# A four-layer graph network on one core: two pools for a strip's weights, an earlier read-back of the in-degrees, another queue for one load, and another layout of four scratch tables

## The chip, the cores and the metric

The kernel runs on one core of a Trainium2 chip. A time is the device time of one execution in microseconds (us); a kernel's time is the median of its runs. The profile is one further execution, with its own time. TensorE is PE in the profile (its weight loads are PEld), VectorE is DVE, ScalarE is ACT, GpSimd is POOL and SyncE is SP. "SPq" and "POOLq" are the queues in which SP and POOL issue DMAs.

## What is computed

6250 nodes with 128 features each, and 206250 directed edges, sorted by destination (100000 pairs in both directions and a loop at each node). Each layer normalises the nodes, sums rows over the edges and adds the result to x:

```python
h = relu(layernorm(x))
x = x + leaky_relu(neighbor @ W1.T + b1 + (h * neighbor) @ W2.T + b2)   # neighbor = sum of edge_weight * h[src] over dst
h = relu(layernorm(x))                                                  # called h1 below
agg = segment_sum(h[src], dst) / maximum(in_degree, 1)
f = gelu(agg @ Wl.T + bl + h @ Wr.T)
x = x + graph_norm(f) + h                                               # one graph: mean and variance over all nodes
h = relu(layernorm(x))
x = x + mean over edges of x_clique @ W.T + b                           # summed over dst, by src
h = relu(layernorm(x))
x = x + GRU(h @ W_in, messages summed over dst) @ W_out + b_out
```

## The kernel before, in words

The graph becomes a dense matrix of counts (how often node s sends to node d), 49 blocks of 128 nodes by 49. It is made once and used in three layers.

**First stage: 25 strips** (`strip`, L857). A strip is two blocks of destinations (256 nodes; the last, number 24, has one block). For each destination the edges' sources and weights are gathered (`prepare`, L637, indirect DMAs on POOL's queue), DVE makes one-hot tiles (L724 to L727), PE multiplies them (L746), and ACT copies two results out: the counts as bytes (`cnt`, L755, then to DRAM as `cnt_d`, L882) and the weighted sums of a strip (`edge_w`, L753, 49 x 256 floats, 50,176 bytes in a partition). `prepare` also counts the in-degrees into `deg` (L678, L685); the last of them comes while strip 23 runs. Layer 0's products of a strip (`layer0`, L775, matmuls L783) run during the next strip; `finish0` (L804) ends layer 0 for a strip and writes three scratch tables: `h_d` (h1), `u_d` (x + h1) and `f_d` (h1 @ Wr.T + bl). For the last strips these writes are on POOL's queue, before that on SP's (L807). Strips 1 to 23 stand inside `tc.manual_schedule()`: each engine takes them in the order of the code. Strip 0 and everything from strip 24 to the end of the first stage stand outside it, and the framework's planner orders their instructions by its own estimate of when each is ready.

**Second to fourth stage: three dense layers** (`dense`, L928, run by L1257 to L1300, inside a second `manual_schedule`). A layer goes through chunks of four blocks of destinations. In layer 1 a chunk takes five loads of `cnt_d` into a ring of three tiles (L954), each feeding two steps; DVE and ACT turn the bytes into floats in `wide` (L966 on DVE, L968 on ACT; both also sum the row into `deg2`), and PE does 98 matmuls into `acc` (L985). Its other operand is h1, split into two parts (`h_parts`). During the first chunk alone, `h_up_to` (L1031) brings h1 from `h_d` by groups of four blocks (13 groups, 256 KB each, three buffers `h`), and DVE splits each group (L587 and L588, "halves"): groups 0 to 2 before the chunk, 3 and 4 ahead of its step q=10, 5 to 7 ahead of q=20, 8 and 9 ahead of q=30, 10 to 12 ahead of q=40.

**Order on the queues at the seam.** Small loads are "chores" between the steps. On SP the second stage begins: the ring's first load (L954), the weight `WlT` (L1051), the in-degrees (`inverse_degrees`, L1056: read `deg_d` back, node by node, 4 bytes each, 6400 of them, and let DVE invert them at L1059 and L1060), h1's groups 3 and 4 (L1035), the ring's second load, and so on. On POOL: two memsets (L1260, L1261). `deg_d` is written from `deg` (3200 runs of 8 bytes) at L910.

**Memory.** The pools of the first stage are closed at its end, and those of the later stages lie over them. Going by the tiles' sizes, the pool `late` (deg2, inv1, WlT, f_sum and others) lies over `keep`, `work` (with finish0's tiles) and the first of the two `edge_w` buffers; the ring lies wholly over the second `edge_w` buffer, which holds the odd strips; `wide` lies over that and the pools after it.

Of the kernel before, what the change touches and what calls it, by code (L numbers as in the profile page):

```python
# [9 lines left out]
F32 = mybir.dt.float32  # L10
# [3 lines left out]
ALU = mybir.AluOpType  # L14
DVE = mybir.EngineType.DVE

P = 128
D = 128
N = 6250
NB = -(-N // P)  # L20
NR = N - (NB - 1) * P
NPAD = NB * P
# [444 lines left out]
SB = 2  # L467
SW = SB * P
STRIPS = [(k, min(SB, NB - k * SB)) for k in range(-(-NB // SB))]
NS = len(STRIPS)  # L470
# [20 lines left out]
def fast(ctx: ExitStack, tc: tile.TileContext, a: dict, out: bass.AP, flag: bass.AP):  # L491


    nc = tc.nc
    const = ctx.enter_context(tc.tile_pool(name="f_const", bufs=1))
    dram = ctx.enter_context(tc.tile_pool(name="f_dram", bufs=1, space=bass.MemoryType.DRAM))
# [3 lines left out]
    make_identity(nc, ident)  # L500
    identh = const.tile([P, P], BF16, name="f_identh")
    nc.vector.tensor_copy(identh, ident)
    ones = const.tile([P, P], F32, name="f_ones")
    nc.vector.memset(ones, 1.0)
    node0 = const.tile([P, NS], F32, name="f_node0")
# [23 lines left out]

    cnt_d = dram.tile([NCH, P, CB, NPR * P], U16, name="cnt_d")  # L530
    cntT_d = dram.tile([P, NQB, NPR * P], U16, name="cntT_d")
    u_d = dram.tile([NPAD, D], F32, name="u_d")
    f_d = dram.tile([NPAD, D], F32, name="f_d")
    h_d = dram.tile([NPAD, D], F32, name="h_d")
    x_d = dram.tile([NPAD, D], F32, name="x_d")
    smp_d = dram.tile([NSMP, 1], I32, name="smp_d")
    deg_d = dram.tile([NS, P, WN], F32, name="deg_d")

    def rows(table, g, nb):
        return table[g * P : (g + nb) * P, :].rearrange("(b p) f -> p b f", p=P)  # L540
# [50 lines left out]
    with ExitStack() as bx:  # L591
        def pool(name, bufs):
            return bx.enter_context(tc.tile_pool(name="b_" + name, bufs=bufs))
# [18 lines left out]

        deg = keep.tile([P, NS, WN], F32, name="deg")
        h0 = keep.tile([P, NB, D], F32, name="h0")
        work, edge = pool("work", 1), pool("edge", 2)
        xpool = pool("x", 2)

        def norms():
# [185 lines left out]
        def finish0(g, nb, agg):  # L804

            w = nb * P
            queue = nc.sync if g < (NS - 3) * SB else nc.gpsimd  # L807
            pt = turned_rows(h0[:, g : g + nb, :], nb)
            inter = work.tile([P, SW], F32, name="inter")
            nc.vector.tensor_mul(by_half(inter, nb), by_half(agg, nb), pt)  # L810
            xs = work.tile([P, SB, D], F32, name="xs0", bufs=2)
            load_x(xs, g, nb)
            yield
            po = banks.tile([P, SW], F32, name="po", tag="pK")
            for j in range(nb):
                s = slice(j * P, (j + 1) * P)
                nc.tensor.matmul(po[:, s], agg[:, s], w1, start=True, stop=False)  # L817
                nc.tensor.matmul(po[:, s], inter[:, s], w2, start=False, stop=True)  # L818
            full = work.tile([P, SW], F32, name="full")
            nc.vector.tensor_add(full[:, :w].rearrange("p (b f) -> p b f", f=D),  # L820
                                 po[:, :w].rearrange("p (b f) -> p b f", f=D), bcast(b12, nb))
            nc.vector.scalar_tensor_tensor(full[:, :w], full[:, :w], 0.2, full[:, :w],
                                           op0=ALU.mult, op1=ALU.max)
            nc.vector.tensor_add(flat(xs[:, :nb, :]), flat(xs[:, :nb, :]), full[:, :w])
            h1 = work.tile([P, SB, D], F32, name="h1")
            yield from norm(xs, h1, nb)
            nc.gpsimd.tensor_tensor(xs[:, :nb, :], xs[:, :nb, :], h1[:, :nb, :], op=ALU.add)
            queue.dma_start(rows(h_d, g, nb), h1[:, :nb, :])
            queue.dma_start(rows(u_d, g, nb), xs[:, :nb, :])
            yield  # L830
            pt = turned_rows(h1, nb)
            ht = work.tile([P, SW], F32, name="ht0")
            nc.scalar.copy(by_half(ht, nb), pt)
            yield
            pf = banks.tile([P, SW], F32, name="pf", tag="pK")
            for j in range(nb):
                s = slice(j * P, (j + 1) * P)
                nc.tensor.matmul(pf[:, s], ht[:, s], wr, start=True, stop=True)  # L838
            fs = work.tile([P, SB, D], F32, name="fs")
            nc.vector.tensor_add(fs[:, :nb, :], pf[:, :w].rearrange("p (b f) -> p b f", f=D),  # L840
                                 bcast(bl, nb))
            queue.dma_start(rows(f_d, g, nb), fs[:, :nb, :])

# [10 lines left out]

        def strip(k, nb):  # L857
            nonlocal before, edges, by_edge, hots
            edge_w = edge.tile([P, NB, SW], F32, name="edge_w")
            end = ends.pop() if ends else iter(())  # L860
            last, piece, following = nb * P // WN, 0, None
            for w0 in range(0, last, PW):
                if w0 % TW == 0:
                    now, t1 = hots, w0 + TW
                    if t1 < last:
                        hots = one_hots(by_edge, t1)
                    elif following:
                        hots = one_hots(following, 0)
                if w0 // PW % PT == PT // 2:
                    if piece in END_AT:  # L870
                        next(end, None)
                    if piece in EDGES_AT:
                        following = next(edges, None)
                if w0 * WN % P == 0:
                    cnt = cnts.tile([P, NPR, P], U16, name="cnt")
                count(w0, now, cnt, edge_w)
                if k and w0 // PW % 2:
                    next(before, None)
                g, w1 = k * SB + w0 * WN // P, w0 + PW
                if w1 * WN % P == 0:  # L880
                    c, i = CHUNK_OF[g]
                    nc.sync.dma_start(cnt_d[c, :, i, :], flat(cnt))  # L882
                if w1 % (PW * PT) and w1 < last:
                    continue
                if not k:
                    next(before, None)
                if piece == NEXT_AT and k + 2 < NS:
                    edges = prepare(k + 2)
                    next(edges)
                for _ in range(TURN_AT.count(piece) if k else 0):  # L890
                    next(turns, None)
                piece += 1
            by_edge = following
            for _ in chain(before, end):
                pass
            before = layer0(k, nb, edge_w)

        strip(*STRIPS[0])
        with tc.manual_schedule():
            for k, nb in STRIPS[1:-1]:  # L900
                strip(k, nb)
        strip(*STRIPS[-1])
        end = ends.pop()
        for _ in before:
# [2 lines left out]
            pass  # L907


        nc.sync.dma_start(deg_d.rearrange("s p w -> p s w"), deg)  # L910
        found = small.tile([P, 1], F32, name="found")
        nc.vector.tensor_reduce(found, deg, axis=mybir.AxisListType.XY, op=ALU.add)
        p_all = psum.tile([1, 1], F32, name="pL")
# [117 lines left out]
    def h_up_to(q):  # L1031
        while to_split and to_split[0][0] < q:
            g, nb = to_split.pop(0)
            h = whole.tile([P, GB, D], F32, name="h")
            nc.sync.dma_start(h[:, :nb, :], rows(h_d, g, nb))  # L1035
            halves(nc.vector, [h_parts[:, g : g + nb, i, :] for i in range(2)], h[:, :nb, :])

    deg2 = late.tile([P, NCH, NB], F32, name="deg2")
    inv1 = late.tile([P, NS * SB], F32, name="inv1")
    wl, wc, w_in, w_msg, w_out = (late.tile([P, D], F32, name="f_" + n)  # L1040
                                  for n in ("WlT", "WcT", "W_inT", "W_msg", "W_outT"))
    w_ih, w_hh = (late.tile([P, 3 * D], F32, name="f_" + n) for n in ("W_ihT", "W_hhT"))
# [10 lines left out]
    def load_row(t, n):  # L1053
        return lambda: nc.sync.dma_start(t, a[n].to_broadcast([P, D]))

    def inverse_degrees():  # L1056
        with nc.allow_non_contiguous_dma(reason="one number for each node, once"):
            nc.sync.dma_start(inv1, deg_d.rearrange("s p w -> (s p w)").rearrange("(b p) -> p b", p=P))
        nc.vector.tensor_scalar(inv1, inv1, 1.0, None, op0=ALU.max)  # L1059
        nc.vector.reciprocal(inv1, inv1)  # L1060

    def load_f(g, nb):
        return lambda: nc.sync.dma_start(f[:, g : g + nb, :], rows(f_d, g, nb))

# [90 lines left out]
    def end2(g, nb, acc):  # L1157
        w = nb * P
# [3 lines left out]
        pa = times(agg, wc, nb)  # L1162
        x = work.tile([P, CB, D], F32, name="x", bufs=3)
        xg, fg = x[:, :nb, :], f[:, g : g + nb, :]
        nc.sync.dma_start(xg, rows(u_d, g, nb))
        nc.gpsimd.tensor_tensor(xg, xg, bcast(b_res, nb), op=ALU.add)
        nc.vector.tensor_mul(fg, fg, bcast(gain, nb))
        yield
# [16 lines left out]
        for _ in steps:  # L1185
            pass
        nc.gpsimd.tensor_tensor(xg, xg, bcast(b_out, nb), op=ALU.add)
        nc.gpsimd.dma_start(rows(x_d, g, nb), xg)
        yield
        pt = psum2.tile([P, CB * P], F32, name="pT")  # L1190
        for j in range(nb):
# [18 lines left out]
    def end3(g, nb, acc):  # L1210
# [23 lines left out]
        new = work.tile([P, CB * P], F32, name="wd")  # L1234
        nc.scalar.activation(new[:, :w], r[:, :w], AF.Tanh, bias=b_ih[:, 2:3])
        x = work.tile([P, CB, D], F32, name="x", bufs=3)
        nc.sync.dma_start(x[:, :nb, :], rows(x_d, g, nb))
        yield
        keep_h = hh[:, cols]
        nc.vector.tensor_sub(keep_h, keep_h, new[:, :w])  # L1240
# [16 lines left out]
    with tc.manual_schedule():  # L1257
        n1 = 2 * NPR // KP
        chores = [[] for _ in range(NCH * n1)]
        chores[0] += [load(wl, "WlT"), lambda: nc.gpsimd.memset(f_sum, 0.0)]  # L1260
        chores[1] += [inverse_degrees, lambda: nc.gpsimd.memset(sq_sum, 0.0)]  # L1261
        for c, (g, nb) in enumerate(CHUNKS):
            chores[c * n1 + (7 if c == 0 else 2)].append(load_f(g, nb))
        for i, g in enumerate(range(0, NQB, GB)):
# [95 lines left out]
```

## Time and profile before

| | us |
|---|---|
| median of 7 runs (lowest 1909.02, highest 1918.71) | 1912.54 |
| the profiled execution | 1916.7 |
| its span, first to last instruction | 1914.9 |
| PE, DVE, ACT, POOL busy | 1796.4, 1409.3, 1205.0, 456.2 |
| first stage: strips and layer 0 | 0 to about 1036 |
| layer 1, first chunk | 1036.8 to about 1071 |
| layer 1, a later chunk | 23.1 each |
| layers 2 and 3 | from about 1350, to the end |

The page gives busy times by engine, 40 slices of the span, DMA queues, the chain of work that ended last, and the costliest groups. Its line numbers are those of the listing above. A busy PE includes time at a lower granted clock, so the clock ("PEclk") has to be read beside it. In an answer by windows, a line has the window, its length, each engine's busy time with the number of instructions, the granted clock, the share of the DMA engines' time and GB/s. A line of waits has the sum, the number of times and the longest.

### The profile page before, as it was taken

What the parts mean: (1) busy time and instruction counts of PE and PEld (TensorE: products, weight loads), DVE (VectorE), ACT (ScalarE), POOL (GpSimd) and SP (SyncE); (2) the same over time, 40 slices, a digit from 0 to 9 for tenths busy, and PEclk for the clock granted to TensorE, in tenths of its full rate; (3) what the DMA queues carried; (4) which work ended last, traced back from release to release, by engine and by line L of the source; (5) the groups of instructions that cost most, each with busy time, mean ns of one, the idle gap of its engine ahead of it and who ended that gap; (6) DMA issues with size and microseconds to landing.
All of it is one profiled execution on the core that took longest, in us unless ns stands there. A gap on an engine that the chain in (4) does not pass through costs nothing.

```text
span 1914.9 us, 65340 instructions
## 1 busy us (share of the span) xinstructions
PE 1796.4 (94%) x28172; PEld 1504.9 (79%) x28172; DVE 1409.3 (74%) x2943; ACT 1205.0 (63%) x2834; POOL 456.2 (24%) x412
## 2 busy tenths in 40 slices
PE   0799999999999999999986999999899999999996
PEld 0688888888888888888875788888677877777774
DVE  5888888888888888888843776776888755444453
ACT  2877777777777777777752676776555554434442
POOL 3134333433343334323401011000523210000000
PEclk9899999999999999999988999999999999999998
DMA  3236454546454645553213654654445454434441
GB/s 74 79 88 135 109 140 100 140 104 134 101 132 106 132 102 130 109 132 86 83 50 87 198 165 137 198 149 123 122 127 149 130 155 141 125 101 151 133 145 46
DMA packets 299742, 232.04 MB, mean 121 GB/s; under 512 B 111184, under 2 KB 288451, under 8 KB 299443
## 3 DMA queue, kind: packets, MB, share of 16 engines
q1 hardware_dynamic: 290627, 213.46, 42.1%
q0 software_dynamic: 7952, 13.91, 2.5%
q8 instruction: 223, 3.65, 0.8%
q10 hardware_dynamic: 864, 0.39, 0.3%
q14 instruction: 76, 0.62, 0.1%
HBM read 130.53 MB, written 76.70 MB: 108 GB/s over the span
## 4 chain that ended last, share of the span: by engine, by line
PE 83%; DVE 7%; issue 4%; DMA 2%; ACT 2%; POOL 0%; SPq 0%; POOLq 0%; DVEq 0%; ACTq 0%
PE acc L985 31%; PE pL L783 29%; PE pK L746 15%; DVE wide L946 1%; PE pf L838 1%; PE po L817 1%; PE pA L1105 1%; DVE x L1175 1%; DVE fh L1132 1%; PE po L818 1%; DMA smp_d<-in_dst 1%; DVE agg L789 1%; ACT h L575 1%; PE pM L1202 0%; PE pA L1247 0%
## 5 line engine op out<-in xcount | busy, mean ns | idle before, releaser
L783 PE MATMUL pL<-edge_w,h 64*128 64x256 f32 (+1 forms) x4900 | 620.3, 388 | 4.7 <-DVE agg L789 1.0
L985 PE MATMUL acc<-wide,parts 128*128 128x512 f32 (+1 forms) x2548 | 583.8, 388 | 11.5 <-DVE wide L966 10.7
L985 PEld LDWEIGHTS acc<-wide,parts 128*128 128x128 f32 x2548 | 464.0, 189 | 116.6 <-issue 14.8
L755 ACT CAST cnt<-pK 128x400 uint8<-128x400 f32 x784 | 396.3, 506 | 204.4 <-PE pK L746 188.6
L783 PEld LDWEIGHTS pL<-edge_w,h 64*128 64x128 f32 x4900 | 436.4, 188 | 46.6 <-DVE agg L789 6.7
L746 PEld LDWEIGHTS <-s_hot 64*128 64x128 bf16 x18816 | 372.8, 95 | 73.2 <-issue 21.1
L746 PE MATMUL pK<-k_hot,s_hot 64*128 64x49 bf16 (+1 forms) x18816 | 389.9, 193 | 24.7 <-ACT edge_w L753 12.5
L753 ACT COPY edge_w<-pK 128x392 f32<-128x392 f32 x784 | 399.1, 509 | 0.0
L727 DVE TENSOR_TENSOR k_hot<-k_hot,by_edge 128x2352 bf16<-128x2352 bf16 x196 | 271.8, 1387 | 8.0
L724 DVE TENSOR_TENSOR s_hot<-iota,keys 128x2048 bf16<-128x2048 bf16 x196 | 239.5, 1222 | 45.6 <-PE pK L746 42.5
L966 DVE TENSOR_SCALAR_CACHE_REDUCE wide<-ring 128x512 fp32r<-128x512 uint8 (+1 forms) x325 | 193.1, 651 | 41.3 <-ACT wide L968 19.3
L968 ACT ACTIVATE wide<-ring 128x512 fp32r<-128x512 uint8 (+1 forms) x312 | 184.9, 596 | 54.7 <-ACT wide L968 32.5
L634 POOL DMA_INDIRECT dst<-in_dst,off_i x50 | 82.6, 1652 | 400.5 <-DVE node L672 383.7
L985 PE MATMUL acc<-wide,q_parts 128*128 128x512 f32 (+1 forms) x650 | 162.0, 399 | 12.8 <-DVE wide L946 12.5
L961 ACT CAST wide<-ring 128x1024 fp32r<-128x1024 uint8 (+3 forms) x130 | 120.9, 957 | 73.9 <-PE acc L985 71.4
L960 DVE CAST wide<-ring 128x1536 fp32r<-128x1536 uint8 (+1 forms) x130 | 119.9, 948 | 54.3 <-PE acc L985 40.7
L985 PEld LDWEIGHTS acc<-wide,q_parts 128*128 128x128 f32 x650 | 116.8, 191 | 44.5 <-DVE wide L946 17.5
L726 DVE TENSOR_TENSOR k_hot<-iota,keys 128x800 bf16<-128x800 bf16 x196 | 126.5, 645 | 0.0
L1251 POOL DMA_DIRECT2D out<-x x12 | 10.2, 851 | 324.0 <-DVE x L1249 324.0
L1230 DVE SCALAR_TENSOR_TENSOR wb<-pT,f_b_hh,wb 128x512 f32<-128x512 f32 (+1 forms) x13 | 9.4, 720 | 100.4 <-PE pT L1227 100.4
L1013 POOL TENSOR_TENSOR f_sum<-f_sum,fh 128x512 f32<-128x512 f32 (+2 forms) x13 | 16.5, 1271 | 279.4 <-ACT fh L1118 237.7
L634 POOL DMA_INDIRECT src<-in_src,off_i x50 | 77.6, 1551 | 15.2 <-issue 14.6
(167 smaller groups left out, 1565.3 us busy)
## 6 DMA issues: line engine op xcount, KB each, us to landing
ring<-cnt_d SPq DMA_DIRECT2D x120, 640.0 KB
cnt_d<-cnt SPq DMA_DIRECT2D x49, 800.0 KB
cntT_d<-tt SPq DMA_DIRECT2D x125, 160.0 KB
ring<-cntT_d SPq DMA_DIRECT2D x60, 320.0 KB
xs<-in_x SPq DMA_DIRECT2D x12, 256.0 KB
xs<-in_x SPq DMA_DIRECT2D x24, 128.0 KB
h<-h_d SPq DMA_DIRECT2D x12, 256.0 KB
fh<-f_d SPq DMA_DIRECT2D x12, 256.0 KB
```

What stands on the lines that cost most here:

```text
L634: nc.gpsimd.indirect_dma_start(out=t, out_offset=None, in_=col[name], in_offset=bass.IndirectOffsetOnAxis(ap=idx, axis=0))
L724: nc.vector.tensor_tensor(s_hot, count_up(P), at(0, P), op=ALU.is_equal)
L726: nc.vector.tensor_tensor(k_hot[:, :, 0], count_up(NBP), at(1, NBP), op=ALU.is_equal)
L727: nc.vector.tensor_tensor(k_hot[:, :, 1:, :NB], k_hot[:, :, :1, :NB].to_broadcast([P, tq, 3, NB, TI]), parts.to_broadcast([P, tq, 3, NB, T ...
L746: nc.tensor.matmul(pk[:, h, to], s_hot[r, u, :, t], rhs, start=j == 0, stop=True, skip_group_check=True)
L753: nc.scalar.copy(m.rearrange("p b (i h) -> p b i h", h=WN), by_block[:, 1, :NB])
L755: nc.scalar.copy(m.rearrange("p b e (i h) -> p b e i h", h=WN), by_block[:, 0].rearrange("p (b e) i h -> p b e i h", e=2))
L783: nc.tensor.matmul(pl[:, h, :w], h0[r, s, :], edge_w[r, s, :w], start=s == 0, stop=s == NB - 1)
L961: nc.scalar.copy(to[:, 3:ks], of[:, 3:ks])
L966: nc.vector.tensor_scalar(to[:, k], of[:, k], 1.0, None, op0=ALU.mult, op1=ALU.add, accum_out=total)
L968: nc.scalar.activation(to[:, k], of[:, k], AF.Copy, accum_out=total)
L985: nc.tensor.matmul(acc[:, : nb * P], parts[:, s, j, :], rhs, start=s + j == 0, stop=s == end and j == 1)
```

## The change

`inv1` moves to the pool of constants, and its read-back to a place ahead of strip 24, outside `manual_schedule`, with the write of `deg_d` in front of it; the chore is gone. The two `edge_w` buffers become two pools of one buffer each, taken in turn. h1's groups are issued by POOL instead of SP. The four scratch tables of nodes by features are laid out partition by partition, `[128, 49, 128]` instead of `[6272, 128]`, so that a transfer of several blocks has one run of 1 KB (two blocks) or 2 KB (four blocks) for each partition, where it had runs of 512 bytes.

```diff
+    inv1 = const.tile([P, NS * SB], F32, name="inv1")
...
-    u_d = dram.tile([NPAD, D], F32, name="u_d")
-    f_d = dram.tile([NPAD, D], F32, name="f_d")
-    h_d = dram.tile([NPAD, D], F32, name="h_d")
-    x_d = dram.tile([NPAD, D], F32, name="x_d")
+    u_d = dram.tile([P, NB, D], F32, name="u_d")
+    f_d = dram.tile([P, NB, D], F32, name="f_d")
+    h_d = dram.tile([P, NB, D], F32, name="h_d")
+    x_d = dram.tile([P, NB, D], F32, name="x_d")
...
-        work, edge = pool("work", 1), pool("edge", 2)
+        work = pool("work", 1)
+        edge = [pool(n, 1) for n in ("edge0", "edge1")]
...
-            queue.dma_start(rows(h_d, g, nb), h1[:, :nb, :])
-            queue.dma_start(rows(u_d, g, nb), xs[:, :nb, :])
+            queue.dma_start(h_d[:, g : g + nb, :], h1[:, :nb, :])
+            queue.dma_start(u_d[:, g : g + nb, :], xs[:, :nb, :])
...
-            edge_w = edge.tile([P, NB, SW], F32, name="edge_w")
+            edge_w = edge[k % 2].tile([P, NB, SW], F32, name="edge_w")
...
         with tc.manual_schedule():
             for k, nb in STRIPS[1:-1]:
                 strip(k, nb)
+        nc.sync.dma_start(deg_d.rearrange("s p w -> p s w"), deg)
+        with nc.allow_non_contiguous_dma(reason="one number for each node, once"):
+            nc.sync.dma_start(inv1, deg_d.rearrange("s p w -> (s p w)").rearrange("(b p) -> p b", p=P))
+        nc.vector.tensor_scalar(inv1, inv1, 1.0, None, op0=ALU.max)
+        nc.vector.reciprocal(inv1, inv1)
         strip(*STRIPS[-1])
...
-        nc.sync.dma_start(deg_d.rearrange("s p w -> p s w"), deg)
...
-            nc.sync.dma_start(h[:, :nb, :], rows(h_d, g, nb))
+            nc.gpsimd.dma_start(h[:, :nb, :], h_d[:, g : g + nb, :])
...
-    inv1 = late.tile([P, NS * SB], F32, name="inv1")
...
-    def inverse_degrees():
...
-        chores[1] += [inverse_degrees, lambda: nc.gpsimd.memset(sq_sum, 0.0)]
+        chores[1].append(lambda: nc.gpsimd.memset(sq_sum, 0.0))
```

The other reads and writes of `u_d`, `f_d` and `x_d` (L841, L1063, L1165, L1188, L1237) change their index in the same way and stay on their queues.

More of the change, by code (lines that the diff above doesn't have):

```diff
@@ L841, in finish0 @@
                                  bcast(bl, nb))
-            queue.dma_start(rows(f_d, g, nb), fs[:, :nb, :])
+            queue.dma_start(f_d[:, g : g + nb, :], fs[:, :nb, :])
         for by_edge in prepare(0):
@@ L1054, in load_row @@
         return lambda: nc.sync.dma_start(t, a[n].to_broadcast([P, D]))
-    def inverse_degrees():
[L1057 to L1060, printed above, removed]
     def load_f(g, nb):
-        return lambda: nc.sync.dma_start(f[:, g : g + nb, :], rows(f_d, g, nb))
+        return lambda: nc.sync.dma_start(f[:, g : g + nb, :], f_d[:, g : g + nb, :])
     q_parts = late.tile([P, NQB, 2, D], F32R, name="q_parts")
@@ L1164, in end2 @@
         xg, fg = x[:, :nb, :], f[:, g : g + nb, :]
-        nc.sync.dma_start(xg, rows(u_d, g, nb))
+        nc.sync.dma_start(xg, u_d[:, g : g + nb, :])
         nc.gpsimd.tensor_tensor(xg, xg, bcast(b_res, nb), op=ALU.add)
@@ L1187, in end2 @@
         nc.gpsimd.tensor_tensor(xg, xg, bcast(b_out, nb), op=ALU.add)
-        nc.gpsimd.dma_start(rows(x_d, g, nb), xg)
+        nc.gpsimd.dma_start(x_d[:, g : g + nb, :], xg)
         yield
@@ L1236, in end3 @@
         x = work.tile([P, CB, D], F32, name="x", bufs=3)
-        nc.sync.dma_start(x[:, :nb, :], rows(x_d, g, nb))
+        nc.sync.dma_start(x[:, :nb, :], x_d[:, g : g + nb, :])
         yield
```

## The prediction, made before the result

> **What bounds the kernel.** I read part 1 of the page first, then the chain that ended last.
>
> ```profile
> PE 1796.4 (94%) x28172; PEld 1504.9 (79%) x28172; DVE 1409.3 (74%) x2943; ACT 1205.0 (63%) x2834; POOL 456.2 (24%) x412
> PE 83%; DVE 7%; issue 4%; DMA 2%; ACT 2%; POOL 0%; SPq 0%; POOLq 0%; DVEq 0%; ACTq 0%
> ```
>
> PE bounds it nearly everywhere. The change takes no work from PE, so it can only win where PE stands or crawls. The slices (part 2) show that once, between strips and layer 1. Asked by windows for the matmuls of L985, the trace gives the first chunk of layer 1 against two later ones (columns: window, length, PE, PEld, clock, DMA share, GB/s):
>
> ```profile
> 1036.00:1071.00 35.00, 27.43 (x98) 20.68 (x99) 0.84 0.76 202
> 1077.00:1100.10 23.10, 22.45 (x99) 18.25 (x99) 1.00 0.56 168
> 1100.10:1123.20 23.10, 22.45 (x100) 18.26 (x99) 1.00 0.56 170
> ```
>
> The same 98 matmuls take 35 us instead of 23.1: the seam loses 12 us there, and 9 us more before it, where PE has nothing from 1027 on but layer 0's tail. The chain, in order of time, names who holds it (start, length, what; one stretch left out):
>
> ```profile
> 1020.53 6.45 PE pL L783 x112
> ...
> 1033.88 1.81 DMA f_d<-fs
> ...
> 1036.81 0.41 SPq L1058
> 1037.27 4.31 SPq L1035
> 1042.17 6.67 DMA ring<-cnt_d
> 1049.62 4.18 PE acc L985 x9
> ```
>
> The chunk opens when f_d of the last strip has landed (1035.69): the tiles in `late` wait for it, WlT on SP and deg2 of L966 included. Then SP issues the read-back (L1058), stands 4.31 us in the first h1 load behind it (the other nine took about 0.36), and issues the ring's second load only at 1042.17; it lands 6.67 us later. DVE's waits from 1036 to 1071, all of them:
>
> ```profile
> DVE inv L1059 <- DMA inv<-deg_d: 3.7, 1, 3.7
> DVE wide L966 <- DMA ring<-cnt_d: 2.7, 1, 2.7
> DVE wide L966 <- DMA f_d<-fs: 2.4, 1, 2.4
> DVE parts L587 <- DMA h<-h_d: 0.4, 1, 0.4
> ```
>
> DVE sets this chunk's pace: 25 casts at 0.605 us from start to start (15.1), nine full splits at 1.07 (0.42 + 0.69, overlapped) and a small one of 0.5 (10.2 together) are 25.3 us, more than PE's 23.1. From 1036.0 to its last cast's end (1069) it took 33. The difference is 3.7 + 2.7 + 0.4 of waits and 0.7 for L1059 and L1060: **7.5 us is the most that can be won here**.
>
> **Part by part.**
>
> *Read-back away from the seam, h1 on POOL's queue* (one account, since either alone leaves the other's delay). SP loses L1058 (0.41), the 4.31 us stand and the h1 issues; the ring's second load goes out right behind WlT, at 1036.8 instead of 1042.2, the third at 1037.4. POOL has nothing between its memset's end (1037.1) and 1078.9 in the trace, so its h1 loads hold up nobody else. One costs it 0.83 us (L1188, also 256 KB, median), against 0.36 on SP. What is late next: from issue to use, h1 took 2.4 us (second load of the pair, issued 1041.6, split 1044.0), so group 3 lands at 1037.1 + 0.8 + 2.4 = 1040.3, where DVE is free at 1039.1: 1.2 us. Group 4 comes 0.8 to 0.9 later, at most 0.6 us late. The ring's second load shares the engines with three h1 groups: 1.43 MB at 287 GB/s, the rate of the window 1056 to 1066, are 5 us, so it lands near 1042.8 where DVE asks at 1042.5: 0.3. Later loads are due seven or more us after their issue. Left over: 2.1 us of waits. Gain 7.5 - 2.1 = **5.4**; PE follows the last cast by 2 us before and after. Bounds: 3.7 (only the read-back's wait goes) and 7.5.
>
> A rule speaks against this queue. The trace's nearest row is POOL's 0.83 us for a 256 KB issue, at a time when DVE was working too. The Trainium skill, page "SBUF — State Buffer", section "SBUF: two separate sides", says that a DMA from POOL's queue cannot get its descriptors written while DVE runs a copy in its fast two-port mode, and that SP's queue is free of this; the page has such a DMA at about 3.1 us instead of 0.62. By the rule the ten splits' copies (L587) could each hold a load; by my rows a copy lasts 0.42 us, so ten of them are 4.2 us at the very most, and most of that falls on loads that are not yet due. I go by the row.
>
> *Read-back in front of strip 24.* Added there: one SP issue, 6400 transfers of 4 bytes, and L1059 and L1060 (0.19 + 0.47) with a wait. The write of deg_d already stood there: the planner had pulled it up to 957.90, as soon as `deg` was whole. Its 8-byte packets ran from 959.4 to 964.0, so the read-back can start at about 965 and, taking the 6.0 us it took before (1036.81 to 1042.82), lands at about 971. SP issues nothing between 958.9 and 974.2, so no other DMA stands behind it. On DVE the one-hots of strip 24 do. How the stretch looks now (timeline; engine, line, idle before in brackets):
>
> ```profile
> 957.90 0.98 SPq L910 DMA_DIRECT2D deg_d<-deg  x1
> ...
> 966.33 0.41 PE L746 MATMUL pK<-k_hot,s_hot 64*128 64x49 bf16 x9 [2.87 <-issue]
> ...
> 967.92 1.23 DVE L724 TENSOR_TENSOR s_hot<-iota,keys 128x2048 bf16<-128x2048 bf16 x1 [5.62 <-PE pK L746]
> ...
> 973.73 0.42 DVE L840 TENSOR_TENSOR fs<-pf,f_bl 128x256 f32<-128x256 f32 x1 [2.61 <-PE pf L838]
> ```
>
> If the planner puts the wait just ahead of L724, DVE resumes there at about 972.1 instead of 967.9; of these 4.2 us, 2.6 are idle time ahead of L840, and some tenths more follow, so about **1.4** reach the chain, which runs through DVE at 974.6. If the wait falls into one of DVE's later gaps (6.6 us idle before 1003.0), it costs nothing; if L724 is needed at once, all 4.2. I take 1.4: where the planner puts deg_d shows that it moves such work up.
>
> The 2.87 us ahead of PE's row is an instruction load: among the trace's DMA packets, PE's loads of 16 KB take 1.0 us (median of 223), and only the one begun at 962.95, in the 8-byte packets' tail, took 4.29. After it the clock stood at 0.50 until 970 and 0.78 until 975, 2.9 us more. Would 6400 packets do it again? At the seam, the smaller loads (8 KB) that fell among the read-back's packets took about 0.5 instead of 0.36. PE loads every five us or so; I charge nothing in the sum and keep 0 to 5.8 us for the range.
>
> The page "Runtime: NRT & Kernel Launch", section "Instruction fetch mechanics", holds that such loads are mostly hidden, since the next page is fetched while this one runs; the 4.29 us row shows one that was not. By the rule this part is nothing.
>
> *Two pools for edge_w.* The ring's first load waited 27.2 us for PE's last products of the stage (issued 1027.06), though its memory is the odd strips', last read at 1010.6. With the split it can go at 1011. But it was early enough already: what opened the chunk was f_d at 1035.69, and behind the ring's first load SP stops at WlT in `late` as before. Gain 0; a loss has no cause, since the two buffers still alternate.
>
> *Layout.* 512-byte packets took 27 to 29 ns, 1280-byte ones 55 to 68 outside the worst crowding: time goes by bytes. Runs of 1 or 2 KB save little DMA time. u_d and x_d are read in layers 2 and 3 well ahead of use (only POOL's add waits, 25 us in ten times, and nobody waited long for it). Issues become a few tenths shorter, beside waits. 0, bounds -1 and +1.
>
> **Sum.** -5.4 + 1.4 = -4.0 us. The profiled execution took 1916.7 (span 1914.9 and 1.8 around it), so it would become 1912.7; it lies 4.2 above the median of the seven runs, all of the difference being elsewhere, so the median goes from 1912.54 to **1908.5**.
>
> **Rivals.**
> 1. *The gain is hidden*: the first chunk stays DVE's, group 3 or the ring's second load comes at 1043 to 1045 because both queues share the engines (DMA share 0.69 to 0.90 there already). Then 3.7 less 1.4 to 3.7: 1910 to 1912.5. For it: those shares. Against: the 4-byte packets, which moved little (102 GB/s at 0.71), are gone.
> 2. *Slower*: the read-back's packets catch a PE instruction load as deg_d's did, at 965 to 971. Price 2.87 standing + 2.9 at a low clock = 5.8, beside DVE's wait of 1.4 to 4.2: 7.2 to 10. It decides as soon as the stall passes 4.0 us; with a gain of 3.7 to 5.4 the time is 1914.3 to 1918.9. For it: twice as many packets as at 962.95. Against: the 8 KB rows.
> 3. *The change frees more than I see*: if the casts no longer had to wait for f_d, up to 9 us (1027.1 to 1036.0) open up: 1901 to 1905. Against: deg2 still lies in `late`.
>
> **Chances and range.** Forecast 0.55 (1905 to 1910.5; 0.40 of it faster by over 0.2%, 0.15 within), rival 1 0.12 (within), rival 2 0.23 (0.20 slower, 0.03 within), rival 3 0.10 (faster). 0.2% is 3.8 us, about what a measurement of this kernel can tell from no change. Together: faster 0.50, same 0.30, slower 0.20. The range runs from the middle of rival 3 to the middle of rival 2: 1903 to 1917.
>
> **What would show it.** Right: SP's second L954 at about 1037, no L1035 on SP, DVE waits of about 2 us in the first chunk, its last cast at about 1063.5, a chunk of 29.5 us; 6400 small packets and a DVE wait of a few us near 965 to 972. Wrong: L985 starting well before 1036, an L1035 issue on POOL of over 2 us, PE idle by "issue" a second time near 970, or a DVE wait on inv1 that PE shows as a standstill.

## The result, and the profile after

The changed kernel takes **1917.50 us** (median of 30 runs, 1914.57 to 1922.43), the kernel before, run beside it, 1914.68 (71 runs): a ratio of 1.0017, 95% interval 1.0011 to 1.0023. It is slower by 2.8 us, some 0.17%: little, but the interval lies clear of 1. Forecast were 4.0 us less. (The 1912.54 that the prediction started from is the median of seven runs; 2.1 us of its miss of 9.0 are this base.)

Part 1 and part 4's first line of the page after, to be set beside those of before:

```profile
PE 1797.1 (94%) x28172; PEld 1503.7 (78%) x28172; DVE 1409.5 (74%) x2943; ACT 1205.7 (63%) x2834; POOL 459.9 (24%) x425
PE 81%; DVE 8%; issue 4%; DMA 4%; ACT 2%; POOL 1%; POOLq 0%; SPq 0%; DVEq 0%; ACTq 0%
```

PE and DVE do no more work to speak of (0.7 and 0.2 us); POOL's 3.7 us more are the h1 issues that it took over. But DMA holds 4% of the chain instead of 2%. Where is told by the chain itself, in order of time (start, length, what; stretches left out):

```profile
957.72 10.65 DMA deg_d<-deg
968.44 5.81 DMA inv<-deg_d
974.96 1.08 DVE s_hot L726
...
1042.03 1.84 DMA f_d<-fs
1045.60 5.15 DMA h<-h_d
1051.28 0.70 DVE parts L589
1052.26 4.99 DMA h<-h_d
```

Two DMAs that the chain of before doesn't hold, the write of deg_d and its read-back, are now on it, one after the other, for 16.5 us. The waits from 930 to 1036 say who stood (engine, what and line, for what: sum, times, longest):

```profile
DVE inv L907 <- DMA inv<-deg_d: 15.1, 1, 15.1
PEld L748 <- DVE k_hot L729: 9.2, 1, 9.2
PE pK L748 <- DVE k_hot L729: 8.5, 1, 8.5
```

DVE stands 15.1 us in the inversion of the in-degrees, and PE 8.5 us behind it, for one-hot tiles that DVE should have made meanwhile. The seam, for its part, did what it should. The matmuls of L991 by windows, the first chunk of layer 1 and a later one (window, length, PE, PEld, clock, DMA share, GB/s), and then all of DVE's waits from 1044 to 1075:

```profile
1044.40:1074.10 29.70, 25.91 (x97) 18.45 (x98) 0.93 0.70 237
1080.00:1103.10 23.10, 22.45 (x99) 18.26 (x98) 1.00 0.55 168
```

```profile
DVE wide L972 <- DMA f_d<-fs: 2.6, 1, 2.6
DVE parts L588 <- DMA h<-h_d: 2.1, 2, 1.5
```

The chunk takes 29.7 us instead of 35, at a clock of 0.93 instead of 0.84. The waits for inv and for the ring are gone, and h is waited for 2.1 us in two waits, where it was 0.4.

To follow a difference through the execution I compare marks: the moments at which one and the same instruction runs in both profiles (ACT's copies of layer 0's sums for the last strips, then ACT's copy of `acc` at the end of each chunk). Where the offset between two profiles steps, time was lost or won.

| mark, us in before | in after | offset |
|---|---|---|
| layer 0's sums, 931.64 | 931.56 | -0.1 |
| 976.46 | 986.20 | +9.7 |
| 1027.03 (last) | 1035.19 | +8.15 |
| first chunk of layer 1, 1071.35 | 1074.58 | +3.2 |
| last chunk of layer 3, 1892.85 | 1895.70 | +2.85 |

Up to the last mark: **+8.2 us** ahead of the seam, **-4.9** in the first chunk, -0.4 over the rest, together 2.9, about the difference of the medians. The agreement is in part chance: behind the last mark the changed kernel's profile is 1.5 us shorter, so that the two profiled executions end only 1.3 us apart (1918.03 and 1916.7).

### The profile page after: what moved, and what is told of

Read it like the earlier page. It is cut to its first block, busy times and chain, and to the rows that moved or that the text cites. A ratio compares the mean times of both kernels' runs of the same rounds, so it can differ in the third digit from the quotient of the medians.

```text
span 1916.2 us, 65358 instructions
## 1 busy us (share of the span) xinstructions
PE 1797.1 (94%) x28172; PEld 1503.7 (78%) x28172; DVE 1409.5 (74%) x2943; ACT 1205.7 (63%) x2834; POOL 459.9 (24%) x425
## 4 chain that ended last, share of the span: by engine, by line
PE 81%; DVE 8%; issue 4%; DMA 4%; ACT 2%; POOL 1%; POOLq 0%; SPq 0%; DVEq 0%; ACTq 0%
PE acc L991 31%; PE pL L785 28%; PE pK L748 14%; DVE wide L952 1%; PE pf L840 1%; PE pA L1104 1%; PE po L819 1%; DVE x L1174 1%; DVE s_hot L726 1%; DVE k_hot L729 1%; DVE fh L1131 1%; PE po L820 1%; DMA deg_d<-deg 1%; DMA h<-h_d 1%; DVE agg L791 1%
## 5 line engine op out<-in xcount | busy, mean ns | idle before, releaser
L991 PE MATMUL acc<-wide,parts 128*128 128x512 f32 (+1 forms) x2548 | 582.2, 387 | 8.1 <-DVE wide L972 7.1
L991 PEld LDWEIGHTS acc<-wide,parts 128*128 128x128 f32 x2548 | 461.7, 189 | 114.0 <-issue 15.0
L972 DVE TENSOR_SCALAR_CACHE_REDUCE wide<-ring 128x512 fp32r<-128x512 uint8 (+1 forms) x325 | 193.0, 650 | 39.1 <-ACT wide L974 19.4
L991 PE MATMUL acc<-wide,q_parts 128*128 128x512 f32 (+1 forms) x650 | 161.9, 399 | 12.4 <-DVE wide L952 12.2
L991 PEld LDWEIGHTS acc<-wide,q_parts 128*128 128x128 f32 x650 | 116.7, 190 | 44.2 <-DVE wide L952 17.0
L1019 POOL TENSOR_TENSOR f_sum<-f_sum,fh 128x512 f32<-128x512 f32 (+2 forms) x13 | 16.5, 1271 | 254.6 <-ACT fh L1117 212.9
```

The source lines that it names most:

```text
L972: nc.vector.tensor_scalar(to[:, k], of[:, k], 1.0, None, op0=ALU.mult, op1=ALU.add, accum_out=total)
L991: nc.tensor.matmul(acc[:, : nb * P], parts[:, s, j, :], rhs, start=s + j == 0, stop=s == end and j == 1)
```

## The experiments

**Theory A**: the loss is DVE's wait for the read-back ahead of strip 24, and the gain at the seam is the read-back's absence there. **Theory B** and other rivals: PE's instruction loads are held up by the small packets, h1's loads by POOL cost or bring something of their own, the pools or the layout do. Each experiment ran in five rounds beside the kernel before, in three sessions: "read-back at the seam" to "only the read-back moved" and "degrees by PE" in one (median of before 1914.92), "only h1 by POOL" to "deg_d by partition" in another (1917.16), the last two in a third (1917.96). Times are compared within a session, ratios across them. The table puts the kernels side by side. Its last three columns are steps of the offset to the profile of before: in the strips' end (marks 931.64 to 1027.03), in the first chunk (to 1071.35), and in the rest. They compare one execution with one, so that a microsecond or two means little; the ratios rest on medians. In the strips' end it is more: the four kernels that write deg_d where it was and read it back at the seam (read-back at the seam, only h1 by POOL, only the pools, only the layout) stand at -2.6 to -6.3 there, so the profile of before is the slowest of five in that stretch.

| kernel | ratio to before, 95% interval | strips' end | first chunk | rest |
|---|---|---|---|---|
| after | 1.0017 [1.0011, 1.0023] | +8.2 | -4.9 | -0.4 |
| read-back at the seam | 0.9987 [0.9978, 0.9997] | -6.3 | -1.3 | +0.7 |
| inversion late | 0.9961 [0.9947, 0.9976] | -3.0 | -5.0 | +1.3 |
| only the read-back moved | 1.0045 [1.0032, 1.0059] | +8.2 | -4.9 | +0.9 |
| only h1 by POOL | 0.9978 [0.9969, 0.9986] | -4.7 | -0.7 | -0.2 |
| only the pools | 1.0004 [0.9996, 1.0013] | -3.7 | -0.5 | +0.4 |
| only the layout | 0.9993 [0.9985, 1.0002] | -2.6 | -0.6 | +1.6 |
| deg_d by partition | 0.9972 [0.9961, 0.9984] | +0.5 | -5.2 | +1.1 |
| degrees by PE | **0.9951 [0.9936, 0.9965]** | -5.6 | -4.1 | +0.2 |
| degrees by PE, rest as before | 0.9956 [0.9938, 0.9974] | -5.9 | -4.6 | +6.4 |
| degrees by PE, h1 by SP | 0.9944 [0.9928, 0.9959] | -7.3 | -4.1 | +5.8 |

### The read-back back at the seam

The changed kernel, with the write of deg_d, the read-back and the inversion where they were before:

```diff
-        nc.sync.dma_start(deg_d..., deg); nc.sync.dma_start(inv1, deg_d...)   # and DVE's two, ahead of strip 24
         strip(*STRIPS[-1])
...
+        chores[1] += [inverse_degrees, lambda: nc.gpsimd.memset(sq_sum, 0.0)]
```

> The changed kernel, but deg_d is written and read back where it was before, as a chore at the seam; pools, POOL's queue for h1 and the layout stay changed. Theory A: the tail is as before (last agg at about 1027), and at the seam the 4-byte read-back stands ahead of the ring's second load on SP again: 1 to 4 us of the 7.5 are won, so 1 to 4 us less than before. Rival B agrees on the tail. Rival C: the tail stays 4 to 8 us late.

0.9987, some 2 us less than before: the loss ahead of the seam is gone, and so is most of the gain behind it (-1.3 instead of -4.9), although h1 is still POOL's. (The -6.3 in the strips' end flatters it: its profile, 1908.17, is the shortest of its twelve runs.) DVE's longest wait at the seam, and SP's issues there (start, length, line), with those of the changed kernel last:

```profile
DVE inv L1060 <- DMA inv<-deg_d: 4.8, 1, 4.8
```

```profile
1030.67 0.38 SPq L1059 DMA_DIRECT2D inv<-deg_d  x1
1031.11 7.04 SPq L956 DMA_DIRECT2D ring<-cnt_d  x3
```

```profile
1044.91 3.20 SPq L960 DMA_DIRECT2D ring<-cnt_d  x3
```

Three ring loads take 3.2 us in the changed kernel, which has no read-back ahead of them, and 7.04 here; the first of them alone 0.57 and 5.65. So SP stands after the read-back whatever is issued next: before, it was an h1 load (4.31 us), here a ring load. The stand is the read-back's, and not h1's.

### Only DVE's inversion late

Both DMAs stay ahead of strip 24; the two DVE instructions go to the seam as a chore:

```diff
-        nc.vector.tensor_scalar(inv1, inv1, 1.0, None, op0=ALU.max)
-        nc.vector.reciprocal(inv1, inv1)
         strip(*STRIPS[-1])
...
+        chores[1] += [inverse_degrees, lambda: nc.gpsimd.memset(sq_sum, 0.0)]   # those two instructions
```

> The changed kernel, but DVE's two instructions on inv1 (maximum and reciprocal) go back to the seam, as a chore of layer 1; both DMAs stay ahead of strip 24. Theory A (DVE, which takes its work in order, stands at the wait for the read-back, and PE runs out of one-hots): the DVE wait of 15.1 us is gone, layer 0's last copy of agg is back at about 1027 (1035.2 in the changed kernel), the first chunk still gains about 5 us, and the kernel takes about 8 us less than the changed one, 5 less than before. Rival B (the small packets themselves hold PE, through its instruction load): the tail stays 4 to 8 us late, and the kernel stays within 4 us of the changed one. Rival C (the planner orders strip 24 worse because of the two pools): the tail stays late too, with no instruction load in the gap.

0.9961, where the changed kernel has 1.0017. All of DVE's waits for a DMA at the seam, where the two instructions now stand:

```profile
DVE wide L970 <- DMA f_d<-fs: 2.6, 1, 2.6
DVE parts L588 <- DMA h<-h_d: 1.6, 3, 0.9
```

There is none for inv, there or ahead of it. The same 9600 packets move at the same place, and the loss is gone: the strips' end is 11.2 us shorter than in the changed kernel (from +8.2 to -3.0), the ratios are 10.7 us apart. It was DVE's wait, not the traffic: Theory A. The traffic has a smaller price, which the next ones show. The chain has it as

```profile
961.68 2.15 issue
```

behind a load of PE instructions that took 3.81 us among deg_d's packets.

### Only the read-back moved

```diff
+        nc.sync.dma_start(deg_d..., deg); nc.sync.dma_start(inv1, deg_d...)   # on the kernel before
+        nc.vector.tensor_scalar(inv1, inv1, 1.0, None, op0=ALU.max)
+        nc.vector.reciprocal(inv1, inv1)
         strip(*STRIPS[-1])
...
-        chores[1] += [inverse_degrees, lambda: nc.gpsimd.memset(sq_sum, 0.0)]
```

> The kernel before with the read-back alone moved ahead of strip 24; one pool, SP's queue for h1 and the old layout. Theory A: tail 8 us late as in the changed kernel; at the seam the read-back's wait of 3.7 and SP's stand of 4.3 are gone, so 3 to 5 us come back: 3 to 5 us slower than before. Rival C: no late tail, faster than before by 3 to 5.

1.0045, 8.5 us slower by the medians, where 3 to 5 were expected. Its chain repeats the changed kernel's loss:

```profile
958.86 10.45 DMA deg_d<-deg
969.33 5.85 DMA inv<-deg_d
```

The step in the strips' end is the same +8.2, and so is the first chunk's -4.9, with h1 on SP and the old memory. **By the profiles' steps, one part of the change makes its whole loss and its whole gain at the seam.** Why its ratio is still 0.3% above the changed kernel's I can't place: in the profiles the steps agree, and the difference is spread (1.0 us from ahead of 931, 1.3 from the rest). The ratios of the four parts alone add up (+0.45, -0.22, +0.04 and -0.07% make +0.20, measured 0.17), so by them, each within its interval, h1 by POOL takes some 4 us off this loss. The profiles don't show them at the seam.

### The other parts alone

Three kernels, each the kernel before with one part: h1's loads by POOL (`nc.gpsimd.dma_start(h...)`), the two pools, the layout of the four tables.

> The kernel before with h1's groups issued by POOL, nothing else. If h1's place on SP behind the read-back is what delays the ring's second load: that load is issued at about 1041 still, behind the 4-byte packets, but h1 does not queue before it, and the first chunk is 1 to 3 us shorter. If the read-back alone matters: no change (within 1 us). If POOL's queue is hurt by DVE's copies: POOL issues of over 2 us each and a chunk as long as before or longer.

> The kernel before with the two edge_w pools alone. Prediction: the ring's first load is issued at about 1011 instead of 1027, and nothing else comes earlier, since f_d's landing opens the chunk: within 1 us of before, but for what the planner reorders in strip 24 (1 to 2 us either way). Rival: if the split frees the casts, the first chunk starts several us earlier.

> The kernel before with the four scratch tables by partition alone. Prediction: within 1 us of before; layers 2 and 3 as long as before (the changed kernel gains 0.4 us between 1071 and 1865). Rival: longer runs free the DMA engines at the seam, and the first chunk is 1 to 3 us shorter.

Pools and layout show no difference, as their intervals hold 1. The pools let the ring's first load go at 1011.27 instead of 1027.06, and the first chunk moved by -0.5. h1 by POOL measures 0.9978, but not where it works: the first chunk moved by -0.7, and DVE waits 5.1 us for inv there instead of 3.7:

```profile
DVE inv L1059 <- DMA inv<-deg_d: 5.1, 1, 5.1
```

Its profile's gain stands in the strips' end, in which it changes no transfer; the stall behind deg_d's packets is 1.13 us in it, 2.87 in before's profile. The five kernels that leave the write and the read-back where they were differ there in just this. From mark 931.64 to mark 976.46 they take 44.8 us (before), 43.8 (layout), 42.7 (pools), 41.7 (h1 by POOL) and 40.1 (read-back at the seam), in the order in which PE stood with nothing to wait for ("issue") between 955 and 975: 3.3, 2.9, 2.6, 1.9 and 1.2 us. I take that for a shift of phase between the packets and PE's instruction loads; it wasn't tried by itself, and why h1 by POOL has the lower median stays open.

### deg_d by partition

If the early read-back is to stay, its chain has to be short. Here deg_d is written as 128 runs of 200 bytes instead of 3200 of 8, and read back by four DMAs:

```diff
-    deg_d = dram.tile([NS, P, WN], F32, name="deg_d")
+    deg_d = dram.tile([P, NS, WN], F32, name="deg_d")
...
-        nc.sync.dma_start(deg_d.rearrange("s p w -> p s w"), deg)
+        nc.sync.dma_start(deg_d, deg)
...
+            for e in range(2):
+                for r in range(2):
+                    nc.sync.dma_start(inv1.rearrange("(p w) (s e) -> p w s e", w=WN, e=2)[:, r, :, e], deg_d[e * H : (e + 1) * H, :, r])
```

> The changed kernel, but deg_d is kept by partition in DRAM, so that its write has 128 runs of 200 bytes in place of 3200 of 8; it is still read back 4 bytes at a time (four DMAs), at the same place, and DVE waits for it there. Theory A in its parts (10.7 us from the write's issue to its landing, 5.8 for the read-back): the write lands in about 2.5 us, DVE's wait falls from 15.1 to 7 to 9 us, layer 0's last agg comes at 1025 to 1029 instead of 1035.2, and PE's instruction load near 962 is no longer slow; 6 to 9 us less than the changed kernel. Rival: landing is slow because the queue is slow there, whatever the runs' size: the wait stays above 12 us and little is won.

0.9972. From its chain, and from the waits from 950 to 1000:

```profile
960.52 2.01 DMA deg_d<-deg
...
966.30 3.20 DMA inv<-deg_d
```

```profile
DVE inv L909 <- DMA inv<-deg_d: 7.6, 1, 7.6
PE pK L748 <- DVE k_hot L729: 5.5, 1, 5.5
```

The same 25 KB land in 2.01 us instead of 10.65. DVE's wait is halved with it, and the step in the strips' end falls from +8.2 to +0.5; the last sums come at 1030.25, where 1025 to 1029 were expected. Of the 223 loads of PE instructions none took over 2 us; in every kernel with the 8-byte write one took 2.9 to 4.3.

### The degrees by PE

Each partition of `deg` holds two neighbouring nodes of every strip, while `inv1` has a block of 128 nodes across the partitions. Four small matmuls with columns of the identity do that move, and DRAM is left out:

```diff
+        for e in range(2):
+            p_inv = banks.tile([P, NS], F32, name="p_inv", tag="pK")
+            for r in range(WN):
+                to = keep.tile([P, H, WN], F32, name=f"to{e}{r}")
+                nc.vector.memset(to, 0.0)
+                nc.vector.tensor_copy(to[:, :, r], ident[:, e * H : (e + 1) * H])
+                nc.tensor.matmul(p_inv, to.rearrange("p a b -> p (a b)"), deg[:, :, r], start=r == 0, stop=r == WN - 1)
+            nc.vector.tensor_scalar(inv1.rearrange("p (s e) -> p s e", e=2)[:, :, e], p_inv, 1.0, None, op0=ALU.max)
+        nc.vector.reciprocal(inv1, inv1)
         strip(*STRIPS[-1])
```

> The changed kernel without deg_d: four small matmuls with copies of the identity's columns bring the in-degrees from deg's order into inv1's, ahead of strip 24, and DVE inverts them there; no DMA. Theory A: no DVE wait of more than a few us, last agg at 1024 to 1028, first chunk shorter by 5: 5 to 8 us less than before, also since the 8-byte packets no longer catch PE's instruction load (2.9 us of standing and 2.9 at a low clock). Rival B: the same, but then e2 is not faster. Rival C: the tail stays late.

**0.9951, the lowest ratio by then, ahead of the kernels before and after.** It is 1904.91 us beside 1908.04 for the late inversion in the same session; their intervals overlap. The timeline shows what stands in for 16.5 us of two DMAs:

```profile
969.26 1.07 PE L909 MATMUL p_inv<-deg,to 128*128 128x25 f32 x8
970.61 0.27 DVE L910 TENSOR_SCALAR inv<-p_inv 128x25 f32<-128x25 f32 x2
```

No load of PE instructions is slow any more, and the strips' end is 5.6 us shorter than in the profile of before. That is close to the 5.8 us at which the prediction priced the held-up load (2.87 standing and 2.9 at a low clock), a cost of that profile which the change left in place. But it is no fixed price: from 931.64 to 976.46 the three kernels without deg_d take 38.8 to 39.1 us, and the five named above 40.1 to 44.8, so the 8-byte write costs 1 to 6 us there. By the two medians (1904.91 and 1908.04) write and read-back together cost about 3 besides DVE's wait, which isn't clear of their intervals. The last sums came at 1020.15, sooner than expected (1024 to 1028).

### The degrees by PE, without the rest of the change

What do h1 by POOL, the pools and the layout bring once the trip through DRAM is gone? One kernel puts the four matmuls into the kernel before and changes nothing else; the other is the kernel above with h1's loads back on SP (`nc.sync.dma_start(h...)`).

> The kernel before with one edit: four small matmuls bring the in-degrees into inv1's order ahead of strip 24, and nothing of them goes through DRAM. h1 stays on SP's queue, one pool of edge_w, the old layout. Theory A (the 6400 descriptors of the read-back are what keeps SP from its next loads, and the other parts of the change bring nothing once they are gone): all that the same matmuls gave on the changed kernel, a ratio of 0.9951 +- 0.0010 (about 1905 beside 1915), the first h1 load on SP issues in under 1 us and the ring's second load by 1.5 us after WlT, and the first chunk ends 4 to 5 us earlier than its start moved. Theory B (h1 has to leave SP for the seam to get shorter): the first chunk gains only 1 to 3 us, ratio 0.9965 to 0.998.

> The kernel with the degrees moved by PE, with h1's loads put back from POOL's queue to SP's (pools and layout as in the changed kernel). Theory A: the same as with POOL's queue within 1 us (0.9951 +- 0.0008), since two h1 issues on SP hold up the ring's second load by about 0.8 us, and the waits of 2 us on h become waits of 1 to 2 us on h or the ring. Theory B: the first chunk is 2 us or more longer, ratio 0.996 or above.

0.9956 and 0.9944: neither can be told from 0.9951. The first chunk gains 4.6 and 4.1 us, with POOL's queue 4.1. On SP, in the first of the two:

```profile
1031.16 0.35 SPq L1058 DMA_DIRECT2D f_WlT<-in_WlT  x1
1031.57 1.32 SPq L1043 DMA_DIRECT2D h<-h_d  x2
1032.94 0.57 SPq L962 DMA_DIRECT2D ring<-cnt_d  x1
```

Two h1 loads take 1.32 us, and the ring's load goes 1.8 us after WlT (I had said 1.5). Nothing stands. DVE's waits at the seam for the ring and for h, in this kernel and then in the one with POOL's queue:

```profile
DVE wide L974 <- DMA ring<-cnt_d: 2.0, 1, 2.0
DVE parts L587 <- DMA h<-h_d: 0.6, 1, 0.6
```

```profile
DVE parts L587 <- DMA h<-h_d: 3.2, 2, 2.2
```

The wait changes its name. Theory A, as far as intervals of about 3 us to either side can tell: once the trip through DRAM is gone, the three other parts may stay or go. The +6.4 and +5.8 in the last column belong to the two profiled executions, each the longest of its kernel's six (1913.65, 1912.08); the section on the hardware comes back to them.

## Why the prediction was wrong, step by step

**The step that failed is the read-back's wait on DVE: 1.4 us forecast (bounds 0 to 4.2), 8.2 measured** against the profile of before, and 10.7 to 11.2 when nothing but the wait is taken out of the changed kernel. It came in the form that the prediction named as a sign of being wrong: a wait on inv1 that PE shows as a standstill (15.1 and 8.5 us). DVE's timeline there (start, length, operation, idle before in brackets), and then the operation of before in front of which the wait now stands:

```profile
974.27 0.19 DVE L907 TENSOR_SCALAR inv<-inv 128x50 f32<-128x50 f32 x1 [15.08 <-DMA inv<-deg_d]
...
974.88 1.16 DVE L726 TENSOR_TENSOR s_hot<-iota,keys 128x2048 bf16<-128x2048 bf16 x1
...
977.86 1.22 DVE L726 TENSOR_TENSOR s_hot<-iota,keys 128x2048 bf16<-128x2048 bf16 x1
...
983.43 0.42 DVE L842 TENSOR_TENSOR fs<-pf,f_bl 128x256 f32<-128x256 f32 x1 [2.38 <-PE pf L840]
```

```profile
959.18 1.22 DVE L724 TENSOR_TENSOR s_hot<-iota,keys 128x2048 bf16<-128x2048 bf16 x1
```

The s_hot at 977.86 is the one that stood at 967.92: 9.9 us late, where I had 4.2. Three errors, all in that one term:

1. *When the read-back lands.* I let it start when deg_d's packets had ended ("about 965") and land at 971; it was issued at 968.44 and landed at 974.27. A write has landed when its DMA reports it, and that was 5.1 us after the last packet (963.2). The trace of before has the packets but no landing of deg_d, since nobody waited soon for it: the row was not there, and I took the packets' end for it instead of bounding it. That is 3.3 us.
2. *Where the planner puts the wait.* I had it ahead of the s_hot at 967.92; it went in front of the one at 959.18, and a whole group of one-hots (974.88 to 977.86, 3.0 us) came behind it too. The planner had pulled deg_d's write up to 957.90 before, and it took the wait on about as early; its estimate of when the read-back would be there isn't on record.
3. *The cover.* I took 2.6 us off for DVE's idle time ahead of `fs`. That idle time was a wait for PE, and PE was waiting for DVE; it moved along and is still there (2.38). Idle time that waits for the delayed chain is no cover.

Of the 9.7 us at the mark 976.46, 1.6 came back: the next stretch (976.46 to 1010.72) took 34.3 us before, at a clock of 0.95, and 32.7 after, at 1.00. That isn't the change's doing, as eight of the ten other profiles take 32.7 to 32.9 there too, whatever they change.

**The seam was right**: -5.4 forecast, -4.9 measured. The ring's second load came from SP behind WlT without a stand; DVE waited 2.1 us for h, as worked out; the chunk took 29.7 us, forecast 29.5. But its account was wrong in one point: "either alone leaves the other's delay". The read-back alone gives it all (only the read-back moved: -4.9), h1 by POOL alone 0.7. I had charged SP's 4.31 us to an h1 load since it stood in that row; it was the read-back's 6400 transfers ahead of it in the queue, behind which a ring load stands as well (5.65 us in the first experiment).

**PE's instruction load**: one was held up as before (from 962.4, 3.58 us, in deg_d's packets), and the read-back caught no other. Its standstill was hidden under PE's wait for DVE. So 0 was right for this term, and rival 2, whose time of 1914.3 to 1918.9 holds the result, has the wrong mechanism: it asked for a second slow load, and the whole loss came from the DVE wait that it had at 1.4 to 4.2. The Trainium skill, page "Runtime: NRT & Kernel Launch", section "Instruction fetch mechanics", holds that such loads are mostly hidden. Between 955 and 975 this fits the kernels without the 8-byte write, in which PE stood 0.4 to 0.6 us by "issue", and not those with it (1.2 to 3.3 us where PE didn't wait for DVE).

**Pools and layout**: 0 each, and so measured. The lock of POOL's queue by DVE's copies that the Trainium skill's page "SBUF — State Buffer", section "SBUF: two separate sides", describes did not show: the ten h1 loads took POOL 0.53 to 0.54 us each, two of them (1050.48 and 1057.43) while a split's copy ran on DVE.

The sum by the measured terms: -5.4 becomes -4.9, +1.4 becomes +8.2, the rest 0 becomes -0.4; -4.0 becomes +2.9.

## What to carry to other kernels

A DMA moved ahead of its old place is early only if what it feeds isn't waited for in order: ask which instruction will wait, what its engine has queued behind it, and whether that engine's idle time is itself a wait for the late chain. Moving the DMA but not the instruction that waits for it ("only DVE's inversion late") kept the gain without the loss. A store and its read-back in turn cost both landings, and a landing has to be taken from a row that has one, not from the last packet. Where a small table only has to change its order between partitions, a few matmuls with columns of the identity did it in 1.07 us of PE and 0.7 of DVE (and 1.4 long before, for the columns), in place of 16.5 us of DMA.

## What the runs showed of the hardware

- **Landing of many small runs.** 25 KB written to DRAM in 3200 runs of 8 bytes landed 10.3 to 10.65 us after their issue (three kernels), in 128 runs of 200 bytes 2.01 us.
- **A queue stands behind many small transfers.** After the issue of 6400 transfers of 4 bytes, SP stood in its next DMA whatever it was: 4.3 to 4.6 us in an h1 load (three kernels), 5.35 and 5.65 in a ring load (two). Without the read-back ahead the same place took 0.41 to 0.95 us.
- **Small packets slow PE's instruction loads.** With the 8-byte write, one load of 16 KB took 2.9 to 4.3 us (median of 223: 1.0), and PE stood for up to 2.9 us at a stretch; with 200-byte runs or none, no load took over 2 us.
- **POOL's issue is longer for short runs**: 0.75 us for 256 KB in runs of 512 bytes, 0.54 in runs of 2 KB.
- **The clock can fall without a standstill.** In the profiles of the last two kernels it was 0.77 from 1700 to 1730, with PE busy 29.25 and 29.41 of 30 us; in eight others it was 1.00 there, in two 0.94. This made the +6.4 and +5.8. Why is open. The windows' answer for the first of the two (DVE, ACT and POOL stand between PEld and the clock here):

```profile
1700.00:1730.00 30.00, 29.25 (x143) 24.64 (x143) 11.36 (x17) 9.07 (x19) 0.75 (x1) 0.77 0.36 111
```
